# First-channel Toeplitz tiles from the filters on chip, one activation table, the filters' bias and frequency on ScalarE

## The chip, the core and the metric

The kernel runs on one core of a Trainium2 chip. A core has TensorE (PE, matrix products into PSUM), VectorE (DVE), ScalarE (ACT), GpSimd (POOL) and SyncE (SP); SP and ACT also issue DMAs, each on a queue of its own, onto the same 16 DMA engines. The metric is the device time of the whole program in microseconds (us).

## What is computed

Four layers act on x of shape (4, 64, 256, 256), float32: four images of 64 channels, each channel a 256x256 plane. Layers 0, 1 and 3 are long convolutions with a kernel of rank one: two small networks with sine activations give, for every channel, one filter along rows and one along columns, and the plane is convolved causally with both. Layer 2 is a Haar transform, a mixing of channels with a soft threshold, and the inverse transform. Cut to what matters here:

```python
h = sin(freq * (z @ w1 + b1))
h = sin(freq * (h @ w2 + b2))
h = sin(freq * (h @ w3 + b3))
h = (h @ wo) * exp(-t * abs(deltas))      # hx from the X weights, hy from the Y weights
y[c] = causal 2-D convolution of x[c] with the outer product hx[:, c] hy[:, c]
out = y + x * bias
```

## The kernel before

A causal convolution along one axis is a product with a Toeplitz matrix. For each channel the kernel holds one SBUF tile `t`, 128 partitions x 2 axes x 256: row p of an axis is the channel's reversed filter, read from p elements further on. `contract` (L189, L190) multiplies a plane with it in four matmuls of 256 columns and four of 128 (the records count two passes for each float32 matmul); `first` does one axis and copies the result from PSUM with ScalarE (L198), `second` does the other and adds bias times input with VectorE (L211).

The filters come first. `filters(layer, queue)` gives the steps of one layer as closures: `load` (L103, L104), three pairs `begin`/`finish` (one matmul, the sine's argument `u` with bias and frequency, its reduction to the interval from -pi to pi on VectorE, then the sine on ScalarE), `end` (the last matmul, the decay, and the write of both axes' filters into the DRAM tensor `pads[layer]`, L135), and `warm`, matmuls whose results are not used. X and Y share one tile: X on partitions 0 to 63, Y on 64 to 127. The list before the event loop runs layer 0 (`one`) and layer 1 (`two`) interleaved by hand; layer 3's filters (`three`) run later as events between the convolutions of the first image. `toeplitz` (L180) reads a channel's tile out of `pads` with one DMA from SP, whose access pattern overlaps: 128 rows of 256, each one element further on.

All later work is a list of events, sorted by tick and place, and emitted in that order; a tile framework keeps one instruction stream for each engine and adds the semaphore waits. In the first stage, image 0's channels go through load, first axis of layer 0, second axis of layer 0, first axis of layer 1, second axis of layer 1, one channel per tick; five tiles `t` rotate. The order on TensorE at the start is: layer 0 first axis of channel 0 (`pa`), its second axis (`py`), layer 0 first axis of channel 1, layer 1 first axis of channel 0, layer 0 second axis of channel 1, layer 0 first axis of channel 2, and so on. After the first image, mixing, inverse transform and layer 3 of one image run beside the convolutions of the next.

The filters' working tiles are cut by `part(n)` out of `z`, the large SBUF tile that holds the coefficients later; the tables of layer 2 (`vts`, loaded at L165) are laid over the same room, so their load waits until the filters' tiles there have been read.

Of the kernel before, what the change touches and what calls it, by code (L numbers as in the profile page):

```python
# [9 lines left out]
F32 = mybir.dt.float32  # L10
F32R = mybir.dt.float32r
AF = mybir.ActivationFunctionType
ALU = mybir.AluOpType
# [3 lines left out]
B, C, S, EMB, ORD = 4, 64, 256, 33, 64  # L17
P = 128
# [14 lines left out]
def ap(t, offset, dims):  # L33
    return bass.AP(tensor=t.tensor, offset=t.offset + offset, ap=dims)
# [3 lines left out]
def conv_seq_kernel(ctx, tc, x, fz, fw, bias, decay, haar, haar_row, factors, vt, taut, wmix, out):  # L38
# [14 lines left out]
    nc = tc.nc  # L53
# [6 lines left out]
    tp = ctx.enter_context(tc.tile_pool(name="toep", bufs=5))  # L60
# [29 lines left out]
    def part(n, parts=P):  # L90
        free[0] += n
        return room[:parts, free[0] - n : free[0]]

    dsb = part(S + 1)

    def filters(layer, queue):

        fz_sb, fw_sb = part(S + P, EMB), part(3 * P + 4)
        par = 3 * P
        st = {}  # L100

        def load():
            nc.sync.dma_start(fz_sb, fz[layer])  # L103
            queue.dma_start(fw_sb, fw[layer])  # L104

        def begin(n):
            ps = bank(f"fp{layer}_{n}").rearrange("p m s -> p (m s)")[:, :S]
            if n == 0:
                nc.tensor.matmul(ps, fz_sb[:, S:], fz_sb[:, :S], start=True, stop=True)
            else:  # L110
                nc.tensor.matmul(ps, fw_sb[:, (n - 1) * P : n * P], st["h"], start=True, stop=True)
            u, k = st["u"], st["k"] = part(S), part(S)
            nc.vector.tensor_scalar(
                u, ps, fw_sb[:, par + n : par + n + 1], fw_sb[:, par + 3 : par + 4], ALU.add, ALU.mult
            )

            nc.vector.tensor_scalar(k, u, INV_2PI, MAGIC, ALU.mult, ALU.add)
            nc.vector.tensor_scalar(k, k, -MAGIC, None, ALU.add)

        def finish(n):  # L120
            u, k, h = st["u"], st["k"], part(S)
            for c in (C1, C2, C3):
                nc.vector.scalar_tensor_tensor(u, k, -c, u, ALU.mult, ALU.add)
            nc.vector.tensor_scalar(u, u, PI_IN, -PI_IN, ALU.min, ALU.max)
            nc.scalar.activation(h, u, AF.Sin)
            st["h"] = h

        def end():
            ps = bank(f"fo{layer}").rearrange("p m s -> p (m s)")[:, :S]
            nc.tensor.matmul(ps, fw_sb[:, 2 * P : 3 * P], st["h"], start=True, stop=True)  # L130
            f = part(ROW)
            nc.vector.memset(f[:, S:], 0.0)
            nc.vector.scalar_tensor_tensor(f[:, :S], ps, dsb[:, S:], dsb[:, :S], ALU.mult, ALU.mult)
            for axis, queue in enumerate((nc.scalar, nc.sync)):
                queue.dma_start(pads[layer][:, axis, :], f[axis * C : (axis + 1) * C])  # L135
            st["f"] = f

        def warm(n):

            ps = psx.tile([P, 2, S], F32, name=f"warm{layer}", tag="mix")  # L140
            for i in range(n):
                nc.tensor.matmul(ps[:, i % 2, :], st["f"][:, :P], st["f"][:, :S], start=True, stop=True)

        steps = [(lambda n=n, do=do: do(n)) for n in range(3) for do in (begin, finish)]
        return [load, *steps, end, warm]

    def constants():
# [10 lines left out]
    def tables():  # L158


        free[0] = S + 1
        vts, fac = (part(2 * 16 * S // 4).rearrange("p (i g k) -> p i g k", i=2, k=16) for _ in range(2))

        def load():
            nc.sync.dma_start(vts[:, 0], vt)  # L165
            nc.sync.dma_start(vts[:, 1], taut)
            nc.sync.dma_start(fac, factors)

        def scale(i):
            nc.vector.tensor_mul(vts[:, i], vts[:, i], fac[:, i])  # L170
            nc.sync.dma_start(
                scales[:, :, i].rearrange("n p g j -> p n (g j)"), vts[:, i].rearrange("p (n g) j -> p n (g j)", g=GT)
            )

        return [load, lambda: scale(0), lambda: scale(1)]

    def toeplitz(layer, c, name):

        t = tp.tile([P, 2, S], F32, name=name, tag="toep")
        nc.sync.dma_start(t, ap(pads[layer], c * 2 * ROW, [[1, P], [ROW, 2], [1, S]]))  # L180
        return t

    def bank(name):
        return psm.tile([P, 2, S], F32, name=name, tag="mm")
# [18 lines left out]
    def second(b, st, key, layer, res, new, tag, ahead=None):  # L203
        def run(c):
            s = st[c]
            if ahead is not None:
                s[ahead] = toeplitz(ahead, c, f"t{ahead}_{b}_{c}")
            ps = bank(f"p{new}_{b}_{c}")
            contract(ps, s[key], s[layer][:, 1, :])
            y = io.tile([P, 2, S], F32, name=f"{new}_{b}_{c}", tag=tag, bufs=BUFS[tag])  # L210
            nc.vector.scalar_tensor_tensor(y, s[res], bsb[:, layer, c : c + 1], ps, ALU.mult, ALU.add)  # L211
            s[new] = y

        return run
# [22 lines left out]
    def convolutions(b, ticks, in_parts=(), border=None):  # L237
# [7 lines left out]
        def load(c):  # L245
            xt = io.tile([P, 2, S], F32, name=f"x_{b}_{c}", tag="in", bufs=3)
            nc.sync.dma_start(xt, x[b, c].rearrange("(k p) w -> p k w", p=P))
            st[c] = {"x": xt, 0: toeplitz(0, c, f"t0_{b}_{c}")}
# [128 lines left out]
    def inverse(b, start, put_off):  # L377
# [12 lines left out]
        def rows(c):  # L390
            a = st[c]["z"]
            ps = psm.tile([P, 2, 2, P], F32, name=f"pw_{b}_{c}", tag="mm")
            for m in range(2):
                nc.tensor.matmul(ps[:, m, 0, :], a[:, 0, m, :], hsinv, start=True, stop=True)  # L394
                nc.tensor.transpose(ps[:, m, 1, :], a[:, 1, m, :], ident)  # L395
            w = mx.tile([P, 2, 2, 2, P], F32R, name=f"w_{b}_{c}", tag="f4")
            nc.scalar.copy(w[:, 0], ps)  # L397
            nc.vector.tensor_tensor(w[:, 1], ps, w[:, 0].bitcast(F32), ALU.subtract)
            st[c]["w"] = w
            if c not in put_off:  # L400
                st[c][2] = toeplitz(2, c, f"t2_{b}_{c}")
# [53 lines left out]
    put_off = range(2, C, 3)  # L455

    one, two, three = filters(0, nc.scalar), filters(1, nc.scalar), filters(2, nc.sync)
    one[0]()
    nc.sync.dma_start(dsb, decay)
    two[0]()  # L460
    nc.sync.dma_start(bsb, ap(bias, 0, [[0, P], [C, 3], [1, C]]))
    for do in (one[1], one[2], two[1], one[3], one[4], two[2], one[5], one[6], two[3], one[7], *two[4:7]):
        do()
    one[8](6)
    two[7]()
    two[8](9)
    for tick, do in enumerate([constants, None, None, *three[:-1], *tables()], 4):
        if do is not None:
            at(tick, 3, lambda unit, do=do: do(), 0)
# [129 lines left out]
```

## Time and profile before

| what | value |
|---|---|
| median of 3 runs | 2987.99 us (2987.79 to 2988.86) |
| the profiled execution's own time | 2989.2 us |
| its span in the profile | 2987.4 us |
| TensorE busy | 2919.9 us, 98% of the span |
| VectorE busy | 2551.9 us, 85% |
| ScalarE busy | 2156.5 us, 72% |
| DMA | 649.72 MB, mean 217 GB/s |
| first convolution matmul starts | 33.90 us |

The span runs from the first to the last record of one profiled execution; 1.8 us of that execution lie outside it, and the median of the runs is 1.2 us below it. "Busy" sums the records of an engine; a matmul's end is modelled. In a timeline the columns are: start, duration, engine (PEld is TensorE's weight load, SPq and ACTq are the issue of DMAs), line, operation, output and input tile, shape, count, and in brackets the idle time of the engine before it with what ended it.

### The profile page before, as it was taken

What the parts mean: (1) busy time and instruction counts of PE and PEld (TensorE: products, weight loads), DVE (VectorE), ACT (ScalarE), POOL (GpSimd) and SP (SyncE); (2) the same over time, 40 slices, a digit from 0 to 9 for tenths busy, and PEclk for the clock granted to TensorE, in tenths of its full rate; (3) what the DMA queues carried; (4) which work ended last, traced back from release to release, by engine and by line L of the source; (5) the groups of instructions that cost most, each with busy time, mean ns of one, the idle gap of its engine ahead of it and who ended that gap; (6) DMA issues with size and microseconds to landing.
All of it is one profiled execution on the core that took longest, in us unless ns stands there. A gap on an engine that the chain in (4) does not pass through costs nothing. (4 is left out here: it accounts for less than half of the span.)

```text
span 2987.4 us, 51999 instructions
## 1 busy us (share of the span) xinstructions
PE 2919.9 (98%) x16950; PEld 2610.5 (87%) x16950; DVE 2551.9 (85%) x4576; ACT 2156.5 (72%) x5005; POOL 0.2 (0%) x4
## 2 busy tenths in 40 slices
PE   7999999999999999999999999999999999999999
PEld 6899988888888888888888988888888988888998
DVE  4766778999998879999989879999998889998776
ACT  1333338999986758989886758989886768887554
POOL 0000000000000000000000000000000000000000
PEclk9999999999999999999999999999999999999999
DMA  4877777766667876676777776676677877777676
GB/s 146 245 234 229 230 231 210 210 200 199 210 201 243 249 219 203 207 209 203 208 213 236 253 224 196 209 211 204 206 211 235 255 238 231 231 232 220 212 210 187
DMA packets 562496, 649.72 MB, mean 217 GB/s; under 512 B 44369, under 2 KB 447412, under 8 KB 562100
## 3 DMA queue, kind: packets, MB, share of 16 engines
q1 hardware_dynamic: 446132, 494.94, 58.0%
q10 hardware_dynamic: 116096, 151.46, 14.2%
q8 instruction: 137, 2.24, 0.3%
q14 instruction: 131, 1.07, 0.1%
HBM read 426.77 MB, written 219.48 MB: 216 GB/s over the span
## 5 line engine op out<-in xcount | busy, mean ns | idle before, releaser
L189 PE MATMUL py<-t,a 128*128 128x256 f32 x3072 | 923.3, 382 | 17.8 <-ACT a L198 8.6
L198 ACT COPY a<-pa 128x512 f32<-128x512 f32 x768 | 473.3, 617 | 442.2 <-PE pa L190 298.2
L190 PEld LDWEIGHTS py<-t,a 128*128 128x128 f32 x3072 | 583.4, 190 | 79.3
L353 ACT ACTIVATE f<-px,vt 128x64 f32<-128x64 f32 x2688 | 589.7, 351 | 75.7 <-DVE f L351 75.3
L190 PE MATMUL py<-t,a 128*128 128x128 f32 x3072 | 590.0, 274 | 0.0
L189 PEld LDWEIGHTS py<-t,a 128*128 128x128 f32 x3072 | 491.6, 191 | 69.5 <-ACT a L198 32.0
L334 PE MATMUL px<-wb,f 128*128 128x256 f32 x2048 | 504.3, 382 | 19.6 <-ACT f L353 19.6
L334 PEld LDWEIGHTS px<-wb,f 128*128 128x128 f32 x2048 | 362.1, 190 | 67.2 <-ACT f L353 32.1
L361 DVE TENSOR_TENSOR mag<-mag,vt 128x1024 f32<-128x1024 f32 x256 | 312.7, 1222 | 18.8 <-ACT mag L359 16.6
L366 DVE SCALAR_TENSOR_TENSOR mag<-mag,f 128x1024 f32<-128x1024 f32 x256 | 312.8, 1222 | 4.4 <-DVE sd L266 0.3
L397 ACT CAST w<-pw 128x512 fp32r<-128x512 f32 x256 | 150.2, 587 | 226.5 <-PE pw L395 214.6
L189 PE MATMUL pa<-t,y 128*128 128x256 f32 x1024 | 306.6, 381 | 2.5 <-DVE y L211 1.6
L189 PE MATMUL pa<-t,x 128*128 128x256 f32 x1024 | 305.6, 380 | 1.5 <-issue 1.5
L359 ACT ACTIVATE mag<-f 128x1024 f32<-128x1024 f32 x256 | 282.9, 1105 | 21.1 <-DVE z L370 7.0
L387 ACT COPY zc<-z 128x512 f32<-128x512 f32 x256 | 282.4, 1104 | 2.3 <-ACT w L397 1.9
L360 ACT ACTIVATE f<-f 128x1024 f32<-128x1024 f32 x256 | 273.2, 1067 | 13.1 <-DVE sd L257 5.7
L278 DVE TENSOR_TENSOR sp<-sd,sp 128x512 fp32r<-128x512 f32 x256 | 176.6, 690 | 92.6 <-ACT sp L277 91.9
L211 DVE SCALAR_TENSOR_TENSOR y<-x,bsb,py 128x512 f32<-128x512 f32 x256 | 191.0, 746 | 55.5 <-PE py L190 48.7
L189 PE MATMUL pa<-t,u 128*128 128x256 f32 x772 | 232.8, 383 | 3.6 <-PE pu L407 3.5
L411 DVE SCALAR_TENSOR_TENSOR t<-r,pu 128x512 f32<-128x512 f32 x256 | 175.0, 684 | 59.4 <-PE pu L407 55.2
L190 PEld LDWEIGHTS pa<-t,x 128*128 128x128 f32 x1024 | 194.6, 190 | 26.3
L190 PEld LDWEIGHTS pa<-t,y 128*128 128x128 f32 x1024 | 194.5, 190 | 26.3
(65 smaller groups left out, 4471.6 us busy)
## 6 DMA issues: line engine op xcount, KB each, us to landing
t<-pad SPq DMA_DIRECT2D x768, 256.0 KB, 4.0
x<-in_x SPq DMA_DIRECT2D x256, 256.0 KB, 3.9
keep<-sd ACTq DMA_DIRECT2D x256, 256.0 KB, 2.9
coef<-co SPq DMA_DIRECT2D x256, 256.0 KB, 3.1
f<-coef SPq DMA_DIRECT2D x256, 256.0 KB, 4.0
r<-keep SPq DMA_DIRECT2D x256, 256.0 KB, 3.2
out_y<-y ACTq DMA_DIRECT2D x256, 256.0 KB, 3.7
late<-u ACTq DMA_DIRECT2D x63, 256.0 KB, 2.8
```

Of the source, the lines that this page charges most:

```text
L189: nc.tensor.matmul(ps[:, m, :], src[:, 0, m * P : (m + 1) * P], t[:, ::-1], start=True, stop=False)
L190: nc.tensor.matmul(ps[:, m, P:], src[:, 1, m * P : (m + 1) * P], t[:, : P - 1 : -1], start=False, stop=True)
L198: nc.scalar.copy(a, ps)
L211: nc.vector.scalar_tensor_tensor(y, s[res], bsb[:, layer, c : c + 1], ps, ALU.mult, ALU.add)
L278: nc.vector.tensor_tensor(w[:, 1], t, w[:, 0].bitcast(F32), ALU.subtract)
L334: nc.tensor.matmul(ps[:, h, q, :], f[:, q, h * P : (h + 1) * P], wb.rearrange("p r n -> p (r n)"), start=True, stop=True,)
L353: nc.scalar.mul(f4[:, j], px[:, j], scale(g, 0)[:, j : j + 1])
L359: nc.scalar.activation(mag, f4, AF.Abs)
L360: nc.scalar.activation(f4, f4, AF.Sign)
L361: nc.vector.tensor_sub(mag, mag, over(g, 1, 16))
L366: nc.vector.scalar_tensor_tensor(mag, mag, 0.0, st[g]["f4"], ALU.max, ALU.mult)
L387: nc.scalar.copy(a, z[:, :, :, c].rearrange("p h (i k) -> p h k i", k=2))
```

## The change

`begin` computes `u` by ScalarE as an activation (Identity, with bias and scale per partition) instead of VectorE's two-operation tensor_scalar; the bias is multiplied with the frequency once per layer after the load (`fb`, a VectorE operation on 128x3). `end` of layers 0 and 1 issues two more DMAs ahead of the writes to `pads`: they write channel 0's tile `t`, one axis from ACT's queue and one from SP's, straight from one partition of the filter tile `f` in SBUF; `toeplitz` hands out that tile for channel 0 and issues no read. A one-column sine on the cleared first column of `dsb` runs before the loads. The matmuls of `warm` go from 6 and 9 to 5 and none.

```diff
     dsb = part(S + 1)
+    direct = {}
 
     def filters(layer, queue):
 
         fz_sb, fw_sb = part(S + P, EMB), part(3 * P + 4)
+        fb = part(3)
         par = 3 * P
         st = {}
 
         def load():
             nc.sync.dma_start(fz_sb, fz[layer])
             queue.dma_start(fw_sb, fw[layer])
+
+            nc.vector.tensor_scalar(fb, fw_sb[:, par : par + 3], fw_sb[:, par + 3 : par + 4], None, ALU.mult)
...
             u, k = st["u"], st["k"] = part(S), part(S)
-            nc.vector.tensor_scalar(
-                u, ps, fw_sb[:, par + n : par + n + 1], fw_sb[:, par + 3 : par + 4], ALU.add, ALU.mult
-            )
+            nc.scalar.activation(u, ps, AF.Identity, bias=fb[:, n : n + 1], scale=fw_sb[:, par + 3 : par + 4])
...
             nc.vector.scalar_tensor_tensor(f[:, :S], ps, dsb[:, S:], dsb[:, :S], ALU.mult, ALU.mult)
+            if layer < 2:
+
+                t = direct[layer] = tp.tile([P, 2, S], F32, name=f"t{layer}_0_0", tag="toep")
+                for axis, queue in enumerate((nc.scalar, nc.sync)):
+                    row = f[axis * C : axis * C + 1]
+                    queue.dma_start(t[:, axis, :], ap(row, 0, [row.ap[0], [1, P], [1, S]]))
             for axis, queue in enumerate((nc.scalar, nc.sync)):
                 queue.dma_start(pads[layer][:, axis, :], f[axis * C : (axis + 1) * C])
...
     def toeplitz(layer, c, name):
 
+        if layer in direct:
+            return direct.pop(layer)
         t = tp.tile([P, 2, S], F32, name=name, tag="toep")
...
     one, two, three = filters(0, nc.scalar), filters(1, nc.scalar), filters(2, nc.sync)
+
+    nc.vector.memset(dsb[:, :1], 0.0)
+    nc.scalar.activation(dsb[:, :1], dsb[:, :1], AF.Sin)
     one[0]()
...
-    one[8](6)
+    one[8](5)
     two[7]()
-    two[8](9)
```

## Prediction

> **What bounds the kernel now.** I read the busy shares first, then stretches of the span, then the timeline of the start, engine by engine. The table of stretches (microseconds, then each engine's busy time with its count, granted clock, DMA share, GB/s):
>
> ```profile
> 0.00:33.90 33.90, 17.03 (x47) 11.53 (x48) 15.96 (x48) 5.44 (x10) 0.20 (x4) 1.00 0.35 107
> 180.00:240.00 60.00, 60.00 (x359) 54.76 (x359) 43.16 (x96) 22.35 (x41) 0.00 (x0) 1.00 0.77 230
> 500.00:2900.00 2400.00, 2359.89 (x13673) 2106.43 (x13674) 2153.98 (x3738) 1918.98 (x4552) 0.00 (x0) 1.00 0.73 218
> ```
>
> From 33.9 us on TensorE is the bound: full from 180 to 240, and 2359.9 of 2400 us later. The change touches the 33.9 us ahead of that; whatever moves TensorE's dense stretch should move the end by as much. So the question is what sets that stretch's start. TensorE's own timeline:
>
> ```profile
> 11.15 1.22 PE L111 MATMUL fp<-z 128*128 128x256 f32 x2 [4.97 <-ACT z L125]
> 15.84 2.08 PE L111 MATMUL fp<-z 128*128 128x256 f32 x4 [3.46 <-ACT z L125]
> 22.02 1.22 PE L130 MATMUL fo<-z 128*128 128x256 f32 x2 [4.11 <-ACT z L125]
> 23.04 1.06 PE L111 MATMUL fp<-z 128*128 128x256 f32 x2
> 23.89 5.00 PE L142 MATMUL warm<-z 128*128 128x256 f32 x12
> 28.73 0.59 PE L130 MATMUL fo<-z 128*128 128x256 f32 x2
> 29.91 4.15 PE L142 MATMUL warm<-z 128*128 128x256 f32 x18 [0.58 <-DVE z L133]
> ```
>
> Up to 22 us TensorE waits for the filters' sines. The unused matmuls fill 29.91 to 34.06, and the convolution starts right behind them: it isn't kept waiting by its tile. That tile's way, on SP's queue and the landing times of the page:
>
> ```profile
> 23.28 0.33 SPq L165 DMA_DIRECT2D z<-in_vt  x1
> 23.80 0.48 SPq L135 DMA_DIRECT2D pad<-z  x1
> 27.62 0.89 SPq L180 DMA_DIRECT2D t<-pad  x2
> 29.88 0.47 SPq L135 DMA_DIRECT2D pad<-z  x1
> 32.29 5.72 SPq L180 DMA_DIRECT2D t<-pad  x4
> ```
>
> Write at 23.80, landed at about 27.6 when the reads go out; channels 0 and 1 of layer 0 land some 4 us later, near 32, and channel 0 of layer 1 near 36. In TensorE's fixed order the later users start at 37.45 (channel 1), 38.76 (layer 1, channel 0), 41.38 (channel 2), 44.00 (layer 1, channel 1). A shift of the dense part is therefore the largest of several: each tile's landing against these marks. ScalarE's part of the delay:
>
> ```profile
> 9.07 0.30 ACT L156 CAST hbr<-hbt 128x128 fp32r<-128x128 f32 x1 [6.14 <-DMA hbt<-in_haar]
> 9.39 1.28 ACT L125 ACT_TABLE_LOAD   x1
> 10.68 0.72 ACT L125 ACTIVATE z<-z 128x256 f32<-128x256 f32 x2
> ```
>
> The first sine's argument is ready at 9.25 us (VectorE's clamp ends there); the cast waiting for a constant, and the table load behind it, hold the sine until 10.68.
>
> **What the Trainium skill says.** (1) "ScalarE: Activation LUTs", section What ACT_TABLE_LOAD costs: about 1283 ns per load; the trace shows exactly 1.28 us. (2) "SBUF — State Buffer", section Door 1: a partition belongs to one of 16 DMA ports, and one port carries about 27.2 GB/s. No transfer in this trace has one partition as its source, so the trace neither confirms nor denies it. (3) "DMA: Bandwidth & Descriptors", section Queues, rings and completion order: each issuing queue has one ring per DMA engine, consumed in order. In the trace the write to `pads` behind the 512 KB load of `in_vt` took 3.8 us to land, against 2.4 for the next one (29.88 to 32.29), which agrees without proving it. (4) "TensorE: Matmul & The Clock Gate", Part 1: TensorE runs at half clock until busy for a window of 3.4 us. The trace agrees: 12 passes of `warm` in 5.00 us (0.42 each), the next 18 in 4.15 (0.23).
>
> **The change part by part.**
>
> *Table and early sine.* One of two loads goes. The early sine sits between the two weight loads on ACT's queue: the second, issued at 1.17 before, now waits for 1.28 us of load and some 0.3 of sine, goes out near 2.8 and lands (2.7 to 3.5 us, from the issue rows) at 5.5 to 6.3. Behind it waits layer 1's `fb` on VectorE, and behind that in program order are layer 0's reduction steps. The load of `dsb` also waits for the sine on SP, with two x loads behind it; `dsb` is needed at 20 us, x near 27: hidden by 10 us.
>
> *u on ScalarE.* VectorE loses 6 x 0.55 us, ScalarE gains 6 times the activation. Rows of the trace with a per-partition scale out of PSUM: 128x64 takes 0.35 us; a 128x1024 activation 1.11; interpolated, 256 columns take 0.50. Bounds 0.42 (the sine of this shape) and 0.60 (the skill's extra 93 ns for a second per-partition operand). Alone it gains nothing on the chain, but VectorE's instructions no longer queue behind the other layer's `u`. `fb` (128x3, not in the trace) is taken at 0.1 us, hidden under the matmul.
>
> *Filters, in sequence.* Layer 0's first reduction resumes at about 6.1 (before: 7.08) and its clamp ends at 8.1 rather than 9.25; the sine starts at once, 8.15 against 10.68: 2.5 us earlier. Next round: matmul 8.6, activation till 10.3, reduction about 2.4 till 12.75, sine, matmul at 13.25 (before 15.84). Third round: both layers' `u` are on ScalarE till 15.85; VectorE needs some 2.4 more for layer 0; sine at 18.35 (before 21.55). The last matmul moves from 22.02 to 18.8 and layer 0's filter is ready at 20.5, not 23.8: **3.3 us earlier**. Layer 1: ScalarE issues two DMAs (0.5 each) ahead of the third `u`, which costs 0.4; five warm matmuls at cold 0.83 end near 25.3; its filter is ready at 26.2, not 29.85.
>
> *The direct tiles.* 128 KiB per axis out of one partition. At 27.2 GB/s that is 4.8 us; the rows start at steps of 4 bytes, and by the skill's account (DMA page, How a descriptor splits) an unaligned 1 KB row costs up to 36 beats instead of 32, so 5.4. I take **5.1**. The bounds of this unknown are 1.0 (nothing special about one partition: half of what 256 KB take beside others in the trace) and 9.6 (a single partition gets half a port). X is first in ACT's ring: issued 20.5, bytes from 21.4, landed near 27.0. Y lies behind `in_vt` (bytes till 22.8): landed 28.4. So channel 0 could start near 27, 7 us earlier. But the queue matters: SP's order now is t0, pad0, t1, pad1, and only then channel 1's read, which before stood ahead of layer 1's write. Waiting for layer 1's filter (26.2) it is issued near 29 and in the ring it stands behind layer 1's direct Y tile, which needs the same port: 22.8 + 2 x 5.1 + 1.0 (both pads, half a us each) = 34.0; plus 1.2 for 256 KB and 0.5 for the receipt: **channel 1's tile lands at 35.7**. Its user stood at 37.45: shift **-1.75**. The other marks are looser: layer 1's X tile near 33 against 38.76; layer 1's channel 1, read after pad1 near 34.5, at 38.5 against 44.00.
>
> *Warm matmuls.* 10 fewer, cover for nothing now. But TensorE, done with channel 0 at about 31, idles nearly 5 us until 35.7, and may fall back to half clock; regaining it costs 1 to 1.7 us, perhaps one time in three: +0.4.
>
> Sum: -1.75 + 0.4 = about -1.4. Rest of the program: the streams have the same order, apart from a few steps of layer 3's filters in a stretch where VectorE and ScalarE have room: nothing. Against the profiled 2989.2 this gives 2987.8; the median stands 1.2 lower, so 2987.99 - 1.4 = **2986.6**.
>
> **The rivals.**
>
> *A fast direct copy* (1 us each). Then channel 1's read is held only by SP's order: issued at 26.2 + 2 x 0.48 = 27.2, landing 4 to 4.3 us later at 31.4: -6.0, so 2982. For it: DMAs here reach 374 GB/s. Against: one partition of 128 must feed everything. Chance 0.25.
>
> *A slow direct copy*, the one on the other side: 9.6 us each. 22.8 + 19.2 + 1.0 + 1.7 = 44.7 against 37.45: **+7.3**, 2995.3. The shift crosses zero where one copy takes 6.0 us, and +6 at 9.0. Speaking for it: 16 engines meet at one partition, and two such copies stand in sequence in SP's ring ahead of a load that TensorE needs. Chance 0.2.
>
> *Nothing gained*: the start moves, but channel 1 arrives as late as before. That is the likely case at copies of 6 us and is contained in its 0.55.
>
> **Numbers.** 0.2% is 6.0 us, about what a measurement of this kernel can tell from no change. The likeliest case (0.55) lies within it. The fast case straddles -6: half of it counts as faster, 0.12. The slow case gives slower 0.2. The rest, 0.68, is the same. Low end: the fast case, 2981.8; high end: the middle of the slow case, 2995.5; the likeliest case's own range is 2984 to 2990.
>
> **What would show it.** Right: one table load; filter of layer 0 written near 20.5; first convolution matmul near 27; then an idle TensorE with channel 1's first axis waiting for `t<-pad` until near 35.7; the direct copies landing 6 us or more after issue. Wrong: the direct copies landing in 3 us, or channel 1's read issued before layer 1's writes; or a sine not moved before 9 us.

## The result and the profile after

The changed kernel takes 2992.75 us (median of 20 runs, 2990.84 to 2995.96) against 2988.35 us (20 runs, 2985.17 to 2991.71): ratio 1.0015, 95% interval 1.0008 to 1.0022. That is 4.4 us slower, with an interval of 2.4 to 6.6 us; the prediction had named 1.4 us faster. The profiled execution of the changed kernel took 2991.04 us with a span of 2988.9 us.

In the rest of this document one point of TensorE's fixed order is **the mark**: the start of layer 0's second axis of channel 1 (`py`), the fifth product of the dense stretch. From there on TensorE runs without a visible gap for tens of microseconds in every kernel shown. Before, it stands at 40.07 us; after, at 44.58 us, 4.5 us later, which is the loss. Before (columns as explained with the timeline above), the first axis of channel 1 and the mark:

```profile
37.45 0.60 PE L189 MATMUL pa<-t,x 128*128 128x256 f32 x2
...
40.07 0.60 PE L189 MATMUL py<-t,a 128*128 128x256 f32 x2
```

TensorE after, in order of time (lines of 128-column products and channel 0's second axis are left out):

```profile
27.02 0.98 PE L132 MATMUL fo<-z 128*128 128x256 f32 x2 [2.62 <-ACT z L127]
30.05 1.22 PE L199 MATMUL pa<-t,x 128*128 128x256 f32 x2 [2.05 <-DMA t<-z]
...
39.49 1.22 PE L199 MATMUL pa<-t,x 128*128 128x256 f32 x2 [2.90 <-DMA t<-pad]
...
42.21 1.06 PE L199 MATMUL pa<-t,y 128*128 128x256 f32 x2
...
44.58 0.60 PE L199 MATMUL py<-t,a 128*128 128x256 f32 x2
```

Two things are to be seen. Channel 0 starts at 30.05, 3.9 us earlier than before, but channel 1 has to wait for its tile until 39.49, which is 2.04 us after its old place at 37.45. And a pair of passes takes 1.06 to 1.22 us until past 43 us, then 0.60: TensorE is at half clock. The table of stretches of the same execution (microseconds, busy time of each engine, then the granted clock, DMA share, GB/s) says it outright:

```profile
30.00:33.00 3.00, 2.93 (x8) 2.27 (x8) 0.00 (x0) 0.00 (x0) 0.00 (x0) 0.50 0.78 28
33.00:36.00 3.00, 2.34 (x7) 1.99 (x8) 0.00 (x0) 0.59 (x1) 0.00 (x0) 0.50 0.77 90
36.00:39.50 3.50, 0.60 (x4) 0.31 (x2) 0.75 (x1) 0.00 (x0) 0.00 (x0) 0.50 0.66 175
39.50:44.50 5.00, 5.00 (x16) 4.28 (x17) 0.00 (x0) 0.59 (x1) 0.00 (x0) 0.51 0.64 159
```

The clock is 0.50 from 30 us to the mark. Channel 1's first and layer 1's first product took 44.58 - 39.49 = 5.09 us, where before the same two took 40.07 - 37.45 = 2.62: 2.47 us more. So 2.04 of late tile and 2.47 of slow clock make the 4.51. The DMA column also shows 28 GB/s between 30 and 33 us at a DMA share of 0.78: the engines are occupied and move little. It is the time of the second pair of direct copies, X's from ACT's queue and Y's from SP's. The queues' packets from 30 to 33 us (q1 is SP's queue, q10 ACT's; packets, MB, share of the 16 engines' time):

```profile
q1 hardware_dynamic: 81, 0.08, 77.3%
q10 hardware_dynamic: 3, 0.00, 0.3%
```

Both copies were issued by 29.1 us, but nearly all that moves is SP's, which is Y's copy. From 23 to 25 us, in the first pair, SP's queue has 49 packets and ACT's none. So the two copies of a pair go for the most part one after the other. Their issue and that of what stands behind them, first SP's queue (start, duration, instruction):

```profile
20.11 0.54 SPq L141 DMA_DIRECT2D t<-z  x1
20.70 0.59 SPq L143 DMA_DIRECT2D pad<-z  x1
28.56 0.51 SPq L141 DMA_DIRECT2D t<-z  x1
29.12 0.59 SPq L143 DMA_DIRECT2D pad<-z  x1
30.31 9.46 SPq L190 DMA_DIRECT2D t<-pad  x4
```

Then ACT's queue, with the activation that stands behind it:

```profile
20.12 0.58 ACTq L141 DMA_DIRECT2D t<-z  x1
20.74 2.80 ACTq L143 DMA_DIRECT2D pad<-z  x1
23.59 0.56 ACT L117 ACTIVATE z<-fp,z 128x256 f32<-128x256 f32 x1 [4.64 <-issue]
```

Layer 0's filter is written out at 20.11, not at 23.80. But X's direct copy, issued at 20.12, is waited for until 30.05, and the two writes to `pads` land at about 30.3, when channel 1's read goes out (before, its read went out by 28.5); that read lands 9.2 us later. And ScalarE sits 2.80 us in the issue of a DMA, so that layer 1's third activation, whose matmul ended near 20.4, runs at 23.59. DMA issues of that time, with KB and us to landing:

```profile
t<-z SPq DMA_DIRECT2D x2, 128.0 KB, 6.7
...
pad<-z SPq DMA_DIRECT2D x2, 96.0 KB, 9.2
pad<-z ACTq DMA_DIRECT2D x2, 96.0 KB, 9.7
```

Before, layer 0's write to `pads` landed 3.6 us after its issue on SP.

### The profile page after: what moved, and what is told of

It reads as the page before. It is cut to its first block, busy times and chain, and to the rows that moved or that the text cites. A ratio compares the mean times of both kernels' runs of the same rounds, so it can differ in the third digit from the quotient of the medians.

```text
span 2988.9 us, 51962 instructions
## 1 busy us (share of the span) xinstructions
PE 2920.1 (98%) x16930; PEld 2610.2 (87%) x16930; DVE 2547.1 (85%) x4571; ACT 2163.4 (72%) x5014; POOL 0.2 (0%) x4
## 5 line engine op out<-in xcount | busy, mean ns | idle before, releaser
L369 ACT ACTIVATE mag<-f 128x1024 f32<-128x1024 f32 x256 | 283.0, 1106 | 20.5 <-DVE z L380 6.7
```

What stands on the lines that cost most here:

```text
L369: nc.scalar.activation(mag, f4, AF.Abs)
```

## The experiments

The differences are against the changed kernel, except in the ninth. The times are medians, with the ratio to the kernel before on the same chip and its 95% interval. Runs 8 and 10 were timed once, which is too little for a ratio.

| run | mark, us | mark - 40.07 | time; before beside it | ratio |
|---|---|---|---|---|
| after | 44.58 | +4.5 | 2992.75; 2988.35 | 1.0008 to 1.0022 |
| 1 no direct copies | 37.85 | -2.2 | 2984.82; 2989.43 | 0.9972 to 0.9988 |
| 2 source spread | 34.22 | -5.9 | 2984.44; 2989.43 | 0.9971 to 0.9989 |
| 3 hold 11 | 43.50 | +3.4 | 2994.46; 2989.43 | 1.0008 to 1.0021 |
| 4 layer 0 only | 40.40 | +0.3 | 2990.04; 2989.43 | 0.9989 to 1.0006 |
| 5 hold 5 | 42.21 | +2.1 | 2992.18; 2989.28 | 1.0001 to 1.0017 |
| 6 no direct, hold 4 | 34.33 | -5.7 | 2981.97; 2989.28 | 0.9966 to 0.9985 |
| 7 early table only | 35.40 | -4.7 | 2983.69; 2989.28 | 0.9976 to 0.9990 |
| 8 other partition | 44.02 | +4.0 | 2990.95 (once); 2989.28 | |
| 9 direct copies alone | 44.70 | +4.6 | 2995.07; 2990.05 | 1.0010 to 1.0028 |
| 10 X alone | 38.04 | -2.0 | 2985.84 (once); 2990.05 | |
| 11 pads on SP | 46.36 | +6.3 | 2995.47; 2990.05 | 1.0009 to 1.0022 |

**1. Without the direct copies.**

```diff
-            if layer < 2:
+            if layer < 0:
```

> The changed kernel without its direct copies: channel 0's tiles are read back from pads as before; one table load, u on ScalarE and the 5 and 0 warm matmuls stay. Theory (the direct copies and what queues behind them cost the time; the filter part is a gain): layer 0's filter is ready near 20.1 us as in the changed kernel, layer 1's near 25.7 (in the changed kernel 28.5, because ScalarE isn't held in a DMA issue); pads lands 3.8 us after its issue, channel 0's tile near 28; channel 1's layer-0 second axis, which starts at 40.07 before and 44.58 after, starts near 34.5 if TensorE keeps its full clock and near 37 if it starts the convolution at half clock. So 3 to 5.5 us faster than before. Rival (u on ScalarE or the early sine makes the start later, or the later stages pay for it): that mark at 40 us or later and a time at or above that of before.

Measured: 0.9980 of before. Layer 0's filter is ready at 19.97, layer 1's at 25.22, channel 0's tile at 27.55, and ScalarE's DMA issue takes 0.52 us instead of 2.80. The filter part is a gain and its rival is out: without the direct copies the kernel is faster than before. The first 9 us of convolution ran at half clock, as the second branch of the expectation said (the mark 37.85, expected near 37); channel 0's first product shows it:

```profile
27.55 1.22 PE L199 MATMUL pa<-t,x 128*128 128x256 f32 x2 [2.84 <-DMA t<-pad]
```

So the half clock does not need the direct copies. It comes with the other part of the change, the cut of the unused matmuls: run 6 puts 4 of them back, and the mark falls by another 3.5 us. The time fell by more (4.6 us in medians) than the mark (2.2); the interval, 3.6 to 8.4, doesn't reach the mark's value. What gave the rest stays open.

**2. Same copies, one source partition per row.** Channel 0's tiles hold other values, so its output isn't the layer's.

```diff
-                    queue.dma_start(t[:, axis, :], ap(row, 0, [row.ap[0], [1, P], [1, S]]))
+                    queue.dma_start(t[:, axis, :], f[:, axis * P : axis * P + S])
```

> The changed kernel with the direct copies of the same size, destination, queues and order, but each row read from a partition of its own (128 source partitions instead of one); channel 0's tiles then hold other values, so the output isn't the reference's. Theory[...]: the copies land within 3 to 4 us instead of 6.7 and 9.9, ACT's next DMA issue takes 0.5 us instead of 2.8, layer 1's filter is ready near 25.9, channel 1's tile lands near 31.5, and the mark of 44.58 comes near 34.5 to 37: 3 to 6 us faster than before. Rival (the number of DMAs and their place in the rings is what costs, whatever their source): copies still land after 6 us or more, ACT's issue stays near 2.8 us, and the time stays 3 to 5 us above before.

TensorE's timeline of this run:

```profile
25.56 0.59 PE L199 MATMUL pa<-t,x 128*128 128x256 f32 x2
...
31.50 0.70 PE L199 MATMUL pa<-t,x 128*128 128x256 f32 x2 [1.55 <-DMA t<-pad]
...
34.22 0.60 PE L199 MATMUL py<-t,a 128*128 128x256 f32 x2
```

Bytes, rows, queues and places in them are those of the changed kernel; the source differs. Channel 0 starts at 25.56 right behind the last filter matmul; channel 1's tile is there at 31.50 instead of 39.49, the copies land in 2.0 to 3.8 us, and the issue of ACT's next DMA takes 0.84 us instead of 2.80. The mark moves by 10.4 us. That the source is what makes the copies slow is thereby shown; the count of DMAs isn't it. One thing is not separated: the 128 rows out of one partition also overlap and start at steps of 4 bytes, and here they don't. The reads of `pads` have such rows too and land 256 KB in a median of 4.0 us before, but out of DRAM.

**3 and 5. Holding TensorE's clock.** 11, then 5, unused matmuls behind layer 1's filter.

```diff
     two[7]()
+    two[8](11)      # run 5: two[8](5)
```

> The changed kernel with 11 warm matmuls after layer 1's filter instead of none, which keep TensorE busy from about 28.5 to 35. Theory (of the 4.5 us by which the mark is late, 2.0 are channel 1's tile landing at 39.5 and 2.5 are TensorE running at half clock after it): channel 0's first convolution moves to about 35, channel 1's still starts at 39.5, but at full clock, and the mark of 44.58 moves to about 42.1; the time falls by about 2.5 us against the changed kernel, to 2 us above before. Rival (the late tile is all, the clock costs nothing): the mark stays near 44.5. Second rival (the later start of channel 0 delays everything): the mark at 46 or later.

> The changed kernel with 5 warm matmuls after layer 1's filter (11 in the run before stood between the halves of channel 0's first product and ended after channel 1's tile had landed). Theory (2.5 of the 4.5 us are TensorE at half clock): channel 0's second axis ends near 39.2, channel 1 starts at 39.5 when its tile has landed, at full clock: the mark (layer 0's second axis of channel 1) at about 42.1 instead of 44.58, some 2 us above before. Rival (the clock costs nothing there): the mark stays at 44.5.

With 11 the unused matmuls were placed between the two halves of channel 0's first product and lasted from 31.90 to about 38; channel 0's second axis was then late itself, and channel 1 started at 40.88 behind it, not at its tile's landing. The mark is 43.50: neither the theory's 42.1 nor the plain rival. Run 5 is the clean one:

```profile
35.31 0.59 PE L199 MATMUL pa<-t,x 128*128 128x256 f32 x2
...
39.49 0.70 PE L199 MATMUL pa<-t,x 128*128 128x256 f32 x2 [1.11 <-DMA t<-pad]
...
42.21 0.60 PE L199 MATMUL py<-t,a 128*128 128x256 f32 x2
```

Channel 1's tile lands at the very same 39.49, and the mark stands at 42.21 instead of 44.58: the half clock was worth 2.4 us at the mark. In the times it doesn't stand out: 2.9 us above before, where the changed kernel is 4.4 above, with intervals that overlap.

**4. The direct copy for layer 0 alone.**

```diff
-            if layer < 2:
+            if layer < 1:
```

> The changed kernel with the direct copy for layer 0's channel 0 alone; layer 1's tile is read from pads. Theory (the second pair of direct copies, standing in SP's ring between layer 0's write and channel 1's read, is what makes channel 1 late): channel 1's read goes out near 30.3, when pads has landed, and lands near 34 instead of 39.5; the mark near 37 at full clock or near 39 at half clock: 1 to 3 us faster than before. Rival (already the first pair's slow landing costs all of it): the mark at 42 or later.

Channel 1's read goes out at 30.53, as expected, and channel 1's first axis follows channel 0 at 36.38 with no wait. But X's tile is again waited for until 30.05 and TensorE runs at half clock from there: the mark is 40.40, and the time is that of before (0.9989 to 1.0006). Without the second pair channel 1 is no longer late. The first pair costs 2.6 us at the mark by itself (run 1, with neither pair, has 37.85), and so what the filter part gains is used up. Both the theory's mark (37 to 39) and the rival's (42 or later) were missed.

**6. No direct copies, the clock held: the version that beats both kernels.**

```diff
-            if layer < 2:
+            if layer < 0:
...
     two[7]()
+    two[8](4)
```

> No direct copies, the filter part as in the changed kernel, and 4 warm matmuls behind layer 1's filter, which fill the 2 us or so until channel 0's tile lands at 27.5. Theory (late tile and half clock are all that cost; the run without direct copies ran its first 9 us of convolution at half clock, which gave back some 4 us): the mark at 33.6 to 34.5 instead of 37.85, so 5.5 to 6.5 us faster than before, and 1 to 4 us faster than the run without direct copies and without warm matmuls. Rival (the earlier start is given back later in the program): the mark moves but the time stays within 2 us of before.

```profile
27.58 0.70 PE L199 MATMUL pa<-t,x 128*128 128x256 f32 x2
...
32.94 0.67 PE L199 MATMUL pa<-t,y 128*128 128x256 f32 x2 [0.23 <-DMA t<-pad]
...
34.33 0.60 PE L199 MATMUL py<-t,a 128*128 128x256 f32 x2
```

2981.97 us against 2989.28, ratio 0.9976 (0.9966 to 0.9985): the mark is 5.7 us earlier, and two tiles arrive almost exactly when they are needed. The reads through DRAM are no hindrance here.

**7. The early table alone.** As run 6, with `u` back on VectorE and without `fb`.

> As the run with no direct copies and 4 warm matmuls, but u back on VectorE: only the early sine (one table load) is left of the filter part. Theory (both parts of it gain, the early table 1.3 to 2 us, u on ScalarE the rest): layer 0's filter ready near 21.5 to 22.5 (before 23.77, with both 19.97), the mark near 36. Rival one (u on ScalarE gains nothing): filter at 20 us. Rival two (the early table gains nothing): filter at 23.7.

Layer 0's filter is ready at 21.30 (before 23.77, run 6 at 20.18), the mark at 35.40. The early sine gains 2.5 us at the filter, `u` on ScalarE another 1.1; neither rival holds.

**8. Y's copies from partition 68.** Channel 0's Y tile holds channel 4's filter.

```diff
-                    row = f[axis * C : axis * C + 1]
+                    row = f[axis * (C + 4) : axis * (C + 4) + 1]
```

> The changed kernel with Y's direct copies reading partition 68 instead of 64 (channel 4's filter, so channel 0's output isn't the reference's). Theory ([...]27 GB/s in all were seen while both copies ran, so partitions 0 and 64 seem to share it): [...]both copies run side by side, X lands near 6.7 us after its issue instead of 9.9, traffic while both run is near 54 GB/s, and channel 1's tile lands near 36. Rival (each DMA engine takes one copy's rows after the other's, whatever the partitions): X still lands after 9 to 10 us and traffic stays near 27 GB/s.

Unclear. Traffic in the stretch from 23 to 26 us is 60 GB/s instead of 37, with 69 packets of ACT's queue beside 112 of SP's (26 beside 87 in the changed kernel), and X's tile is waited for until 29.21 (9.1 us after its issue, against 9.9): some of the theory. But in the second pair, from 30 to 33 us, it is 27 GB/s as with partition 64, all 80 packets are SP's, and channel 1's tile comes at 39.93. The expectation took the 27 GB/s of the changed kernel for both copies' rate; there too nearly all packets of that stretch were SP's. Whether two single-partition copies from suitable partitions can run side by side throughout is left open.

**9. The kernel before with the direct copies alone.** The edit is the `direct` part of the change, put into the kernel before; everything else, warm matmuls too, is as before.

> The kernel before with the direct copies alone (filter part, table loads and 6 and 9 warm matmuls as before). Theory (the four copies take some 19 us in sequence from layer 0's filter on, and only then channel 1's tile is read; the filter part of the change hid 3.7 us of that): layer 0's filter at 23.8, channel 1's tile landing near 43.2, the mark near 45.8 at full clock (the 9 warm matmuls stand behind channel 0's first half product) or 48 at half clock, so 5.5 to 8 us slower than before. Rival (the copies cost only beside the new filter part): the mark near 40 to 42, within 2 us of before.

Mark 44.70, ratio 1.0019 (1.0010 to 1.0028), 5.0 us in medians: slower, as the theory says, a little less than its 5.5 to 8. The rival is out, but the theory's path isn't what occurred. X's tile is waited for from 28.5 to 33.04, the 9 warm matmuls then run between the halves of channel 0's first product until 39.2, and channel 1 follows at 42.08 without a wait for its tile, which was there earlier than the 43.2 expected. Here channel 0's late tile sets the mark, with the warm matmuls behind it.

**10. X from one partition, Y spread.** Channel 0's Y tile holds other values.

```diff
-                    queue.dma_start(t[:, axis, :], ap(row, 0, [row.ap[0], [1, P], [1, S]]))
+                    queue.dma_start(t[:, axis, :], f[:, P : P + S] if axis else ap(row, 0, [row.ap[0], [1, P], [1, S]]))
```

> The changed kernel with X's direct copies from one partition as they are and Y's from 128 partitions (channel 0's Y tile then holds other values, so the output isn't the reference's). It measures one such copy alone. If one source partition gives 27 GB/s and the two copies shared that rate: X alone takes 4.8 us of bytes and lands about 6 us after its issue, traffic near 27 GB/s while it runs alone, channel 1's tile lands near 34. If a copy out of one partition is bound by itself at half of that: X lands after 9 to 10 us as in the changed kernel, traffic alone near 14 GB/s, channel 1's tile near 36 or later.

TensorE's first product, the stretch in which the second X copy runs by itself, and the packets of SP's and ACT's queues in that stretch:

```profile
27.40 1.22 PE L199 MATMUL pa<-t,x 128*128 128x256 f32 x2 [1.65 <-DMA t<-z]
...
28.00:32.00 4.00, 3.33 (x14) 2.68 (x13) 0.00 (x0) 0.58 (x1) 0.00 (x0) 0.67 0.80 27
...
q10 hardware_dynamic: 104, 0.11, 79.8%
q1 hardware_dynamic: 2, 0.00, 0.1%
```

One copy alone moves 27 GB/s, not 14, and its tile comes 7.3 us after the issue (20.12), not 9.9: as to the rate of one copy, the first branch holds. Channel 1's tile comes at 35.32, between the two branches. But the two copies did not share that rate: the 28 GB/s of the changed kernel were one copy's as well, and the other waited. The packets show more. No one-partition copy stands in SP's queue in this run, and yet hardly anything of SP's moves while ACT's copy runs: SP's write to `pads`, issued at 26.84, lands 6.9 us later, where run 2 has 2.4. A slow copy holds up the other queue too.

**11. All writes to `pads` of layers 0 and 1 from SP.**

```diff
-            for axis, queue in enumerate((nc.scalar, nc.sync)):
+            for axis, queue in enumerate((nc.sync if layer < 2 else nc.scalar, nc.sync)):
```

> The changed kernel with all writes to pads of layers 0 and 1 issued from SP, so that ScalarE isn't held 2.8 us in the issue of a DMA behind a slow copy. Theory: ScalarE's third activation of layer 1 starts near 21.4 instead of 23.59, layer 1's filter is ready near 26.3 instead of 28.53; the copies' total bytes stay the bound, so channel 1's tile still lands between 37.5 and 39.5 and the mark comes between 42 and 44.6: 0 to 2.5 us faster than the changed kernel, still not faster than before. Rival (the held ScalarE is the cause of the lateness): channel 1's tile lands by 36.5 and the mark is at or below 40.

SP's queue of this run:

```profile
20.71 6.55 SPq L143 DMA_DIRECT2D pad<-z  x2
27.36 4.90 SPq L141 DMA_DIRECT2D t<-z  x1
32.30 4.22 SPq L143 DMA_DIRECT2D pad<-z  x2
```

ScalarE is free: layer 1's filter is ready at 25.40 instead of 28.53. But the hold has only moved to SP, which now sits 6.55, 4.90 and 4.22 us in its issues; the tile of channel 1 comes at 41.08, and the mark is the latest of all, 46.36. Freeing ScalarE by itself doesn't help while the slow copies stay; the theory's "0 to 2.5 us faster" is wrong too.

## Why the prediction was wrong, point by point

- **What bounds, and that the start decides: right.** Moving the mark by 4.5 us moved the median by 4.4; in the other runs the two differ by up to 2.4 us (run 1).
- **The filters: right, and somewhat better.** Predicted for layer 0's filter 20.5, measured 20.08; first sine 8.15 against 7.58. Two guesses were off without harm: the second weight load went out at 1.23, during the table load instead of behind it; the activation took 0.56 us, not 0.50 (inside 0.42 to 0.60).
- **Layer 1's filter: wrong.** Predicted 26.2, measured 28.53. The step "ScalarE issues two DMAs (0.5 each)" failed: the second issue lasted 2.80 us behind the slow copy. Run 2 gives 0.84 and run 1 gives 0.52 for it. Run 11 frees ScalarE, with layer 1's filter at 25.40, and gains nothing; but it holds SP instead, so what the hold alone costs was not separated, its share in the early drop of the clock included.
- **The direct copies: the step that failed.** The working let X and Y run side by side at one port's rate each, 5.1 us per copy, and counted only Y's two copies, 22.8 + 2 x 5.1, ahead of channel 1's read. The rate of one copy was right (27 GB/s in run 10); the overlap was wrong. The copies of a pair went mostly one after the other, and what stood in the other queue waited as well. So X's tile was waited for until 30.05, not 27.0; ScalarE was held in its next issue, and layer 1's filter, with it the second pair, came 2.3 us later than predicted; and channel 1's read met X's second copy, whose queue had 45.5% of the engines' time from 35.5 to 37.5 us. Predicted 35.7, measured 39.49: 3.8 us, which turns -1.75 into +2.04. How the 3.8 us divide among these was not separated. Two figures of the working had no support: no line shows the 0.5 us for the receipt, and "up to 36 beats" is about the mean that the cited rule gives over rows at steps of 4 bytes, with 40 as its most. Neither decides.
- **The unused matmuls and the clock: the second step, mis-sized.** "10 fewer, cover for nothing now" and "perhaps one time in three: +0.4" stood for 2.47 us in the changed kernel, 2.4 in run 5's comparison and 3.5 between runs 1 and 6. The prediction let the clock drop in the idle time after channel 0. It was at half already before channel 0 (the trace grants 0.50 from about 27.3 on), and in run 1 as well, without direct copies. Of the statement on the clock the trace before bears out the two speeds, not the 3.4 us: TensorE had work from 22.02 us on without a gap, and the 12 `warm` passes from 23.89 to 28.89 still took 0.42 us each.
- **The queue's order: right.** Channel 1's read did stand behind layer 1's direct copies in SP's ring, and run 4, which takes these away, removes its wait. But SP's own queue is not the whole of it: in run 10 no such copy stands ahead of the read there, and it still took from its issue at 27.96 to 35.32.
- **The rivals.** The slow copy came nearest: it had named the side and the place, with a per-copy rate of half a port and +7.3 us. What occurred is the full rate for a copy, but one copy at a time for most of the way. The fast copy (-6.0) is what run 2 shows, at -5.9 on the mark and with channel 1's tile at 31.50 (31.4 in the working), once the source has 128 partitions. Its chance of 0.25 and the slow one's 0.2 stood on an argument that no line of the trace could decide.

The Trainium skill's statement that decided the price ("SBUF — State Buffer", section Door 1: some 27 GB/s through one port) agrees with the 27 GB/s of run 10. That partitions 0 and 64 lie on two different ports didn't give two such rates at once: from 30 to 33 us, with both copies issued, 28 GB/s moved, nearly all of it Y's.

## What to carry to other kernels

A DMA that builds an on-chip tile out of one partition saves the way through DRAM and pays with the rate of its one source: price it by source partitions, not by bytes against the full rate. Count two such copies one after the other unless a trace shows that they overlap, and count everything that is queued meanwhile, in the other queue too, the issuing engine included. When the start of a dense stretch is moved, follow every later user's tile, not the first one's, and ask whether the tensor engine is still at full clock when the tiles come. A few unused matmuls that bridge the wait can be worth several microseconds (4 of them 3.5 us at the mark, run 6 against run 1), and where they stand in the order decides whether they help.

## What the runs showed of the hardware that was not expected

- One source partition: 27 GB/s for one copy of 128 rows of 1 KB (run 10); from 128 partitions copies of the same size land in 2.0 to 3.8 us (run 2).
- Two such copies, from partitions 0 and 64 and from two queues, went mostly one after the other: 81 packets of one against 3 of the other from 30 to 33 us in the changed kernel. While one ran alone, the other queue's writes waited too: 104 packets against 2 from 28 to 32 us in run 10. Why the engines serve one queue so long is open.
- The issue of a DMA is not a fixed half microsecond: behind slow copies it held ScalarE 2.80 us (0.52 without them, run 1), and SP 6.55 us for two (run 11).
- The issue of a DMA on ACT's queue at 1.23 us ran beside the table load (1.16 to 2.44 us) and did not wait for it.
